# Three edits to a two-block convolution kernel: how a band table reaches both halves of SBUF, when the first normalisation reads its PSUM bank, and where three tables are cleared

## The chip, the cores and the metric

The kernel runs on one core of a Trainium2 chip. The metric is the device time of one execution in microseconds (us). The kernel before takes 5860.17 us, the median of three runs (5853.47 to 5860.35 us). All arithmetic is in 32-bit floats.

## The reference

The input `x` has 8 images of 96 x 96 pixels with 192 channels. Two residual blocks follow each other, each behind a group normalisation over 32 groups of 6 channels:

```
def _gn(v, G=32, eps=1e-5):            # per image and group, over rows, columns and 6 channels
    return (g - mean(g)) / sqrt(var(g) + eps)

# block 0: 192 -> 384 channels, 3x3 depthwise, four running averages, layer norm, 384 -> 192
proj  = einsum(_gn(x), W_in) + b_in
local = depthwise_conv3x3(proj, conv_w)
mixed = 0.25*(lr + rl + tb + bt) + local   # s = 0.6*s + 0.4*x along columns and rows, both ways
x = x + einsum(layernorm(mixed), W_out) + b_out

# block 1: 7x7 depthwise, layer norm, 192 -> 768 -> gelu -> 192
y = depthwise_conv7x7(_gn(x), dw_kernel) + dw_bias
y = einsum(gelu(einsum(layernorm(y), w0) + b0), w1) + b1
x = x + y * gamma
```

## The kernel before, in words

The program goes through five stages, A to E. Between them everything lies in HBM (the tensors `P_d`, `M_d`, `X1_d`, `X2_d`, `Y_d`). Inside each stage the order of the instructions on every engine is the order in which the source issues them (`tc.manual_schedule()`); tile pools decide which buffer a tile gets, and an instruction waits until the former user of that buffer is done.

**Stage A** (group norm 0 and the projection). It has 8 images of 12 steps each. A step transposes four pairs of image columns on TensorE (`turn`, L351, three times per step: k = 0, 2, 1), scales them on the way out of PSUM (ScalarE L358 for k = 0 and 2, VectorE L356 for k = 1), multiplies with `W_in` in `project_full` (twelve matmuls, L365) and `project_rest` (twelve, L378), and evicts with the bias (ScalarE L391, VectorE L389). While image b is projected, VectorE collects the statistics of image b+1 (`bn_stats`, L320). In the last steps of an image the statistics are finished by `norm_steps`, whose closures are taken one by one by the table `ends`: `means` in step 9 after `project_full`, `squares` in step 10 after `project_full`, `powers` and `shift` in step 10 after `project_rest`, then `spread` and `keep` in step 11. The small results of `norm_steps` lie in a PSUM bank (`gn_ps`) of the same pool and tag as the transposes (`pt`), and that tag has two banks. `means` writes the bank (L51, L52); it is read at the beginning of `squares` (L57, L59). `squares` writes a bank (L71); it is read at the beginning of `powers` (L75).

Image 0 has nothing to hide behind: its statistics and `norm_steps` run ahead of the first step. In step 3 of image 0 `spread_kernels` builds the band tables of the two depthwise convolutions in SBUF: GpSimd clears `z0`, `z1` and `pad` (L265, L276, L290), VectorE copies the taps in (L267, L284), TensorE transposes the 7x7 taps (L274), VectorE takes them out (L275). In step 4 `store_kernels` stores the three tables on SyncE's queue (L293, L298, L299). The memory of `pad` and its neighbours is used again by stage C's constants, whose first write (`mean_w`, L791, VectorE) therefore waits until the stores have landed.

**Stage B** does the 3x3 convolution by banded matmuls (L582) and the running averages (VectorE scans, L612 and L621). **Stage C** does layer norm and `W_out`, adds the residual, and collects the statistics of group norm 1; it calls the same `norm_steps`, whose closures are there taken one per step, from a pool tag of its own with one bank.

**Stage D** (the 7x7 convolution). Channels are handled in 32 blocks m of 6; an iteration i takes the two blocks 2i and 2i+1. `load_d(m)` brings two things:

- `xin`: three times two transfers of 64 partitions x 6 KB (L753), the even ones (partitions 0 to 63) on SyncE's queue, the odd ones (64 to 127) on GpSimd's;
- `band`: the banded taps, the same 64 rows for both halves of the partitions, so one transfer of 64 partitions x 1248 floats on each queue (L758).

Five blocks fit in SBUF (`ND` = 5), so block m's load waits for the matmuls of block m-5. `scale_d(m)` applies group norm 1 to `xin` in eight VectorE instructions (L1016). `conv_d` does 432 matmuls an iteration (L1031) from both halves of the partitions, and ScalarE evicts (L1042). `store_d` stores the result, partitions 0 to 63 on SyncE's queue and 64 to 127 on GpSimd's (L1068). The order in an iteration i is: store of i-1 on SyncE's queue; loads of blocks 2i+3 and 2i+4; store of i-1 on GpSimd's queue; `scale_d` of 2i+2 and 2i+3; the matmuls of i.

**Stage E** is layer norm and the two dense layers, with the result.

Of the kernel before, what the change touches and what calls it, by code (L numbers as in the profile page):

```python
# [28 lines left out]
    nc.gpsimd.tensor_tensor(out, t, neg_half[:rows, :n], ALU.pow)  # L29


def norm_steps(nc, pool, psum, tag, st, avg, count, neg_half):

    rows, n, k, _ = st.shape
    sub = 2 * k
    sv = st.rearrange("p n k (e t) -> p n (k e) t", t=3)  # L40
    rb = pool.tile([n, 2], F32, tag="gn_rb", name="gn_rb")
    t = {}

    def bank():
        return psum.tile([128, 512], F32, tag=tag, name="gn_ps")

    def means():
        ms = pool.tile([rows, n], F32, tag="gn_ms", name="gn_ms")
        nc.vector.tensor_reduce(ms, sv[:, :, :, 1], AX.X, ALU.add)
        t["ps"] = ps = bank()  # L50
        nc.tensor.matmul(ps[:, :n], avg, ms, start=True, stop=True)  # L51
        nc.tensor.matmul(ps[:n, n : n + 1], ms, avg[:, 0:1], start=True, stop=True)  # L52

    def squares():

        gm = pool.tile([rows, n], F32, tag="gn_gm", name="gn_gm")
        nc.vector.tensor_scalar(gm, t["ps"][:rows, :n], 1.0 / sub, None, ALU.mult)  # L57
        t["mean"] = mean = pool.tile([n, 1], F32, tag="gn_mean", name="gn_mean")
        nc.vector.tensor_scalar(mean, t["ps"][:n, n : n + 1], -1.0 / sub, None, ALU.mult)  # L59
        d = pool.tile([rows, n, sub], F32, tag="gn_d", name="gn_d", bufs=1)  # L60
        nc.vector.tensor_tensor(
            d, sv[:, :, :, 1], gm.unsqueeze(2).to_broadcast([rows, n, sub]), ALU.subtract
        )
        nc.vector.tensor_tensor(d, d, d, ALU.mult)
        nc.vector.scalar_tensor_tensor(
            d, sv[:, :, :, 2], 1.0 / count, d, ALU.mult, ALU.add
        )
        ds = pool.tile([rows, n], F32, tag="gn_ds", name="gn_ds")
        nc.vector.tensor_reduce(ds, d, AX.X, ALU.add)
        t["ps"] = ps = bank()  # L70
        nc.tensor.matmul(ps[:n, 0:1], ds, avg[:, 0:1], start=True, stop=True)  # L71

    def powers():
        ve = pool.tile([n, 1], F32, tag="gn_ve", name="gn_ve")
        nc.vector.tensor_scalar(ve, t["ps"][:n, 0:1], 1.0 / sub, GN_EPS, ALU.mult, ALU.add)  # L75
        nc.gpsimd.tensor_tensor(rb[:, 0:1], ve, neg_half[:n, 0:1], ALU.pow)

    def shift():
        nc.vector.tensor_tensor(rb[:, 1:2], t["mean"], rb[:, 0:1], ALU.mult)

    return [means, squares, powers, shift], rb


@with_exitstack
def conv_blocks_kernel(
# [83 lines left out]
    nc.vector.memset(avg, 1.0 / S)  # L169
    neg_half = const.tile([128, 64], F32, name="neg_half")  # L170
    nc.vector.memset(neg_half, -0.5)
    ones = const.tile([64, 128], F32, name="ones")
    nc.vector.memset(ones, 1.0)


# [47 lines left out]
    with ExitStack() as ph:  # L223
# [14 lines left out]
            nc.scalar.dma_start(bin_, b_in.rearrange("(m p) -> p m", p=128))  # L238


        member = cp.tile([GROUPS, 2, GROUPS, GS], F32, name="member")
        for i in range(2):
            nc.vector.tensor_copy(
                member[:, i],
                ident[:GROUPS, :GROUPS].unsqueeze(2).to_broadcast([GROUPS, GROUPS, GS]),
            )
        memberf = member.rearrange("p i g s -> p (i g s)")

# [6 lines left out]
        pad = zp.tile([S, D * WV * B // S], F32, name="pad")  # L255

        def load_kernels():
            nc.sync.dma_start(
                k0.rearrange("p m a b -> p m (a b)"),
                conv_w.rearrange("(m p) o a b -> p m (o a b)", p=128),  # L260
            )
            nc.sync.dma_start(k1, dw_kernel.rearrange("a b o c -> (a b) (o c)"))

        def spread_kernels():
            nc.gpsimd.memset(z0, 0.0)  # L265
            for m in range(NC):
                nc.vector.tensor_copy(  # L267
                    z0[:, m, :, RB - 1 : RB + 2],
                    k0[:, m],
                )  # L270
            kps = ps_t.tile([128, 512], F32, tag="pt", name="kps")
            for i in range(2):
                half = kps[:S, i * 64 : i * 64 + 49]
                nc.tensor.transpose(half, k1[:, i * S : (i + 1) * S], ident[:49, :49])  # L274
                nc.vector.tensor_copy(k1t[:, i].rearrange("p a b -> p (a b)"), half)  # L275
            nc.gpsimd.memset(z1, 0.0)  # L276
            for i in range(2):
                for p in range(PH):
                    for d in range(3):

                        kw = d * PH + p - 2
                        lo, hi = max(0, -kw), min(PH, 7 - kw)
                        if lo < hi:
                            nc.vector.tensor_copy(  # L284
                                z1[:, i, p, d * ZS + ZO : (d + 1) * ZS].rearrange(
                                    "c (t e) -> c t e", e=PH
                                )[:, :, lo:hi],
                                k1t[:, i, :, kw + lo : kw + hi],
                            )
            nc.gpsimd.memset(pad, 0.0)  # L290

        def store_kernels():
            nc.sync.dma_start(  # L293
# [21 lines left out]
        def stats_a(b):  # L315

            st = sp.tile([S, GROUPS, NK, 6], F32, tag="gn_st", name="gn_st")

            def step(k, g):
                nc.vector.bn_stats(  # L320
                    st[:, g, k],
                    xq[b * NK + k].rearrange("p j w c -> p (j w) c")[:, :, g * GS : (g + 1) * GS],
                )

            last, rb = norm_steps(nc, sp, ps_t, "pt", st, avg, NJ * WA * GS // 2, neg_half)
            cols = sp.tile([128, 3, 2], F32, tag="cols", name="cols")
            held = []

            def spread():
                ps = ps_t.tile([128, 512], F32, tag="pt", name="ps_col")  # L330
                for k, lo in enumerate((0, 128, DH)):
                    nc.tensor.matmul(
                        ps[:, 2 * k : 2 * k + 2],
                        memberf[:, lo : lo + 128],
                        rb,
                        start=True,
                        stop=True,
                    )
                held.append(ps)

            def keep():
                nc.vector.tensor_copy(cols.rearrange("p k a -> p (k a)"), held[0][:, 0:6])

            bn = [lambda k=k, g=g: step(k, g) for k in range(NK) for g in range(GROUPS)]
            return bn, last + [spread, keep], cols
# [394 lines left out]
    def load_d(m):  # L740
        c = m * HC
        row = D * WV * B
        pool = d_pools[m % ND > 0]
        xin = pool.tile([128, NT, BP, HC, 2 * WV], F32, tag="xin", name="xin")

        for t in range(NT):
            for g, eng in enumerate((nc.sync, nc.gpsimd)):
                src = bass.AP(
                    tensor=X1_d.tensor,
                    offset=X1_d.offset + (2 * t + g) * HG * PH * row + c * WV * B,  # L750
                    ap=[[row, 64], [1, HC * WV * B]],
                )
                eng.dma_start(  # L753
                    xin[g * 64 : (g + 1) * 64, t].rearrange("q a c n -> q (a c n)"), src
                )
        band = pool.tile([128, HC, ZW], F32, tag="band", name="band1")
        for g, eng in enumerate((nc.sync, nc.gpsimd)):
            eng.dma_start(  # L758
                band[g * 64 : (g + 1) * 64].rearrange("q c l -> q (c l)"),
                Z2_d[:, c : c + HC].rearrange("r c l -> r (c l)"),  # L760
            )
        return band, xin

    s1 = s1_pool.enter_context(tc.tile_pool(name="s1", bufs=1)).tile(
# [2 lines left out]
    with ExitStack() as ph:  # L767
# [108 lines left out]
        def group_steps(x1c, k, i):  # L876
# [16 lines left out]
            steps = [bn[j : j + per] for j in range(0, len(bn), per)]  # L893
            if n < NH * NS - 1:
                return steps
            last, rb = norm_steps(nc, sp, ps_s, "gn_ps", st, avg, GS * WC // NS // 2, neg_half)
            held = []

            def spread():

                dg = sp.tile([2 * GROUPS, 2, 2 * GROUPS], F32, tag="gn_dg", name="gn_dg", bufs=1)
                for a in range(2):
                    nc.vector.tensor_scalar(
                        dg[:, a],
                        ident[: 2 * GROUPS, : 2 * GROUPS],
                        rb[:, a : a + 1],
                        None,
                        ALU.mult,
# [1 line left out]
                ps = ps_s.tile([128, 512], F32, tag="gn_ps", name="ps_s1")  # L910
                nc.tensor.matmul(
                    ps[:, : 4 * GROUPS],
                    ones[: 2 * GROUPS],
                    dg.rearrange("p a g -> p (a g)"),
                    start=True,
                    stop=True,
# [81 lines left out]
    with ExitStack() as ph:  # L998
# [9 lines left out]
                dw_bias.rearrange("(i k c) -> k i c", k=2, c=HC)[k].partition_broadcast(64),  # L1008
            )

        def scale_d(m, xin):
            xv = xin.rearrange("q t a c (v b) -> q t a c v b", b=2)
            for b in range(B):
                sc, sh = (s1[:, a, b % 2, b // 2, m : m + 1] for a in range(2))
# [59 lines left out]
        with tc.manual_schedule():  # L1074
            loads = [first_d] + [load_d(m) for m in range(1, 3)]
            make_weights(ps_y.tile([128, 512], F32, tag="py1", name="ps_b0"))
            for m in range(2):
                scale_d(m, loads[m][1])
            done = None
            for i in range(n_i):  # L1080
                pair, loads = loads[:2], loads[2:]
# [7 lines left out]
                    store_d(done, i - 1, 1)  # L1089
                if i + 1 < n_i:  # L1090
                    for k in range(2):
                        scale_d(2 * i + 2 + k, loads[k][1])
                done = op.tile([128, NB, BP * NV, HC, 2 * WQ], F32, tag="yo", name=f"yo_{i}")
                for c in range(HC):
                    conv_d(pair, c, done, i)
# [248 lines left out]
```

## Time and profile before

The profiled execution took 5861.74 us and has a span of 5860.0 us, so 1.7 us lie around the span. The stages below are stretches of its span; PE busy is TensorE's busy time, DMA the mean busy share of the core's 16 DMA engines, clock the share of TensorE's clock that was granted.

| stage | stretch, us | PE busy, us | clock | DMA | GB/s |
|---|---|---|---|---|---|
| A | 45 to 783 | 714.0 | 0.99 | 0.84 | 245 |
| B | 798 to 1831 | 1025.1 | 0.99 | 0.91 | 236 |
| C | 1831 to 2874 | 1015.5 | 0.99 | 0.92 | 272 |
| between C and D | 2874 to 2904 | 8.3 | 0.50 | 0.88 | 268 |
| D, first iteration | 2904 to 2950 | 27.9 | 0.73 | 0.93 | 265 |
| D, loads running | 2950 to 3336 | 331.4 | 0.93 | 1.00 | 322 |
| D, end | 3336 to 3400 | 46.8 | 0.89 | 0.68 | 212 |
| E, start | 3400 to 3460 | 28.9 | 0.66 | 0.58 | 130 |
| E | 3460 to 5860 | 2392.1 | 1.00 | 0.26 | 69 |

How to read it: where PE busy is close to the stretch, TensorE sets the pace and only what stands in its queue counts; where it is not, and the DMA share is 1.00, the transfers set it. Matmuls are pipelined, so a busy TensorE need not be at its peak. In the lines further down "PE", "PEld", "DVE", "ACT", "POOL" and "SPq" are TensorE's matmuls, its weight loads, VectorE, ScalarE, GpSimd and SyncE's queue; the numbers in front are the start and the busy time in us; the bracket gives the idle time before, and what ended it. KB are 1024 bytes.

### The profile page before, as it was taken

The page shows a single profiled execution, that of the slowest core. Times are in us where ns is not written, and L with a number is a line of the kernel's source. Part 1 is how long each engine was busy: PE and PEld are TensorE (multiplying, and loading weights), DVE is VectorE, ACT ScalarE, POOL GpSimd, SP SyncE. Part 2 cuts the span into 40 slices and gives each one's busy share as a digit, 9 for nine tenths or more (in the row PEclk, how much of TensorE's full clock was granted, in tenths as well). Part 3 has the DMA queues.
Part 4 walks back from the last instruction along what each step waited for, and adds up shares of the span by engine and source line. Part 5 has one row for each costly group of instructions (what it writes and reads, how often), then busy time and mean ns, then how long its engine had stood idle before and what let it go on. Part 6 is the DMA issues. An engine that isn't in the chain of part 4 may idle for free.

```text
span 5860.0 us, 123059 instructions
## 1 busy us (share of the span) xinstructions
PE 5592.6 (95%) x48550; PEld 3974.4 (68%) x48550; DVE 3452.2 (59%) x8023; ACT 2426.3 (41%) x6146; POOL 2560.5 (44%) x2731
## 2 busy tenths in 40 slices
PE   6999989999998999999688869999999999999999
PEld 3655533333335999999677757777777777777777
DVE  5556459999996777777633234444444444444443
ACT  2444447777775666666344422222222222222222
POOL 1111138888886777777422223333333323333322
PEclk9999989999999999999899989999999999999999
DMA  7999879999997999999899942323222232323221
GB/s 206 275 286 257 233 202 244 243 243 243 244 244 207 268 276 282 277 282 276 255 316 327 298 120 60 80 65 81 64 68 74 64 81 65 80 65 78 63 64 40
DMA packets 634284, 1054.50 MB, mean 180 GB/s; under 512 B 108683, under 2 KB 509284, under 8 KB 633708
## 3 DMA queue, kind: packets, MB, share of 16 engines
q1 hardware_dynamic: 516924, 620.81, 40.4%
q0 software_dynamic: 110656, 423.20, 22.6%
q8 instruction: 385, 6.31, 0.5%
q10 hardware_dynamic: 6128, 2.61, 0.2%
q14 instruction: 191, 1.56, 0.1%
HBM read 585.19 MB, written 476.72 MB: 181 GB/s over the span
## 4 chain that ended last, share of the span: by engine, by line
PE 77%; DMA 6%; issue 1%; DVE 1%; SPq 1%; POOL 1%; ACT 0%; POOLq 0%; ACTq 0%; DVEq 0%
PE po L1233 19%; PE po L835 13%; PE hp L1203 13%; PE pl L582 10%; PE hp L1213 7%; PE pa L603 5%; PE pt L833 4%; DMA xin<-X_d 2%; PE pa L606 2%; PE py L1031 2%; PE pt L1186 2%; DMA Y_d<-yo 2%; DMA band<-Z_d 1%; DMA X_d<-x1c 0%; SPq L1068 0%
## 5 line engine op out<-in xcount | busy, mean ns | idle before, releaser
L1222 ACT ACTIVATE g<-hp,b0g 128x384 f32<-128x384 f32 x1152 | 563.3, 587 | 1834.3 <-PE hp L1213 1834.3
L1233 PE MATMUL po<-w1g,g 128*128 128x192 f32 x6912 | 1162.6, 327 | 0.0
L1233 PEld LDWEIGHTS po<-w1g,g 128*128 128x128 f32 x6912 | 1121.5, 190 | 1.1 <-issue 1.1
L835 PE MATMUL po<-wc,mt 128*96 128x193 f32 x4608 | 883.5, 327 | 0.0
L1190 DVE COPY yT<-pt 128x384 f32<-128x384 f32 x288 | 248.5, 863 | 1043.9 <-PE pt L1186 1043.5
L1203 PE MATMUL hp<-yT,w0w 128*128 128x384 f32 x2304 | 781.8, 489 | 0.4 <-DVE yT L1190 0.4
L1251 POOL DMA_DIRECT2D out_dram<-xo x576 | 342.6, 597 | 878.3 <-DVE xo L1240 863.5
L835 PEld LDWEIGHTS po<-wc,mt 128*96 128x96 f32 x4608 | 713.1, 164 | 3.2 <-DVE x1u L858 0.5
L582 PE MATMUL pl<-pin,band 34*32 34x380 f32 (+1 forms) x13824 | 629.8, 489 | 18.9 <-DMA pin<-P_d 18.5
L1203 PEld LDWEIGHTS hp<-yT,w0w 128*128 128x128 f32 x2304 | 429.6, 191 | 257.5 <-issue 3.7
L612 DVE TENSOR_TENSOR_SCAN z<-decay,loc 128x768 f32<-128x768 f32 x288 | 505.8, 1756 | 60.5 <-ACT loc L591 30.8
L652 POOL TENSOR_TENSOR mo<-mo,z 128x768 f32<-128x768 f32 x288 | 529.7, 1840 | 3.4 <-ACT mo L607 0.4
L29 POOL TENSOR_TENSOR rs<-rs_ve,neg_half 96x8 f32<-96x8 f32 x96 | 159.1, 1657 | 822.6 <-DVE rs_ve L28 804.6
L582 PEld LDWEIGHTS pl<-pin,band 34*32 34x32 f32 x13824 | 232.7, 107 | 397.9 <-issue 397.6
L621 DVE TENSOR_TENSOR_SCAN z<-decay,z 128x768 f32<-128x768 f32 x288 | 498.2, 1730 | 0.0
L1031 PE MATMUL py<-xin,band 63*64 63x248 f32 (+1 forms) x6912 | 406.1, 389 | 81.3 <-DVE xin L1016 50.7
L842 ACT ACTIVATE sq<-pt,mean 96x384 f32<-96x384 f32 x768 | 443.0, 577 | 25.7 <-ACT mean L839 0.8
L1031 PEld LDWEIGHTS py<-xin,band 63*64 63x64 f32 x6912 | 348.5, 140 | 138.6 <-DVE xin L1016 40.1
L603 PE MATMUL pa<-loc,mix 128*32 128x384 f32 x3456 | 431.9, 493 | 0.0
L606 PE MATMUL pa<-last,down 96*32 96x384 f32 x1152 | 426.8, 493 | 1.0 <-ACT mo L607 1.0
L1213 PE MATMUL hp<-yT,w0w 64*128 64x384 f32 x2304 | 423.5, 500 | 0.0
L365 PE MATMUL pm<-xT,win 128*128 128x384 f32 x1152 | 397.4, 496 | 5.1 <-DVE po L389 5.1
(116 smaller groups left out, 7623.8 us busy)
## 6 DMA issues: line engine op xcount, KB each, us to landing
P_d<-po POOLq DMA_DIRECT2D x96, 1152.0 KB, 9.9
pin<-P_d SPq DMA_DIRECT2D x192, 576.0 KB
mt<-M_d SPq DMA_DIRECT2D x576, 192.0 KB
xq<-in_x_dram SPq DMA_DIRECT2D x96, 576.0 KB
xr<-in_x_dram SPq DMA_DIRECT2D x384, 144.0 KB
X_d<-x1u POOLq DMA_DIRECT2D x192, 288.0 KB, 4.5
X_d<-x1c SPq DMA_DIRECT2D x192, 288.0 KB
y<-Y_d SPq DMA_DIRECT2D x24, 2304.0 KB
```

The source lines that it names most:

```text
L582: nc.tensor.matmul(pls[g][at * RB : (at + 1) * RB, :, lo:hi], band[rows, c, kh, :], pin[rows, c, :, NJ - 1 - j, lo + kh - 1 : hi + kh - 1] ...
L603: nc.tensor.matmul(pa[at], mix[:, i, at], loc[:, q], start=True, stop=True)
L606: nc.tensor.matmul(pa[at], down[:, to], last[:, q], start=True, stop=True)
L612: nc.vector.tensor_tensor_scan(zf, decay_f, loc.rearrange("p q n -> p (q n)"), 0.0, ALU.mult, ALU.add)
L621: nc.vector.tensor_tensor_scan(zr, decay_f, zr, 0.0, ALU.mult, ALU.add)
L652: nc.gpsimd.tensor_tensor(m, m, z, ALU.add)
L835: nc.tensor.matmul(po[:S, b], lhs[m], wc[:, m], start=(m == 0), stop=(m == NC - 1))
L1031: nc.tensor.matmul(pys[t // 2][g][k * 64 : (k + 1) * 64, t % 2, :, lo:hi], pair[k][0][rows, c, d * ZS : d * ZS + 64], pair[k][1][rows, t, ...
L1203: nc.tensor.matmul(hps[m, q], w0w[:, 2 * q, m * 128 : (m + 1) * 128], yT[:, 2 * q], start=True, stop=False,)
L1213: nc.tensor.matmul(hps[m, q], w0w[p, 1, m * 128 : (m + 1) * 128], yT[p, 1], start=False, stop=True,)
L1222: nc.scalar.activation(g[:, m, q], hps[m, q], AF.Gelu, bias=b0g[:, m : m + 1], scale=1.0)
L1233: nc.tensor.matmul(po[:, q], g[:, m, q, k * 128 : (k + 1) * 128], w1g[:, m], start=(m == 0), stop=(m == NE - 1),)
```

## The change

1. **Band rows.** `load_d(m)` issues one band transfer in place of two: into partitions 0 to 63 on SyncE's queue where m is even, into 64 to 127 on GpSimd's queue where m is odd. The other half of the partitions is filled by one VectorE copy at the head of `scale_d(m)`.
2. **`norm_steps`.** The reading of the bank becomes closures of its own (`take_means`, `take_squares`). With `at_once` they run directly behind the matmuls that fill the bank (stage A); without it they run where they ran before (stage C). Besides, the small tiles get 128 rows or columns in place of 32 or 64 (`rb`, `ms`, `ds`, `mean`, `ve`, `member`, `ones`, `gn_dg`), with the unused columns of `ms` and `ds` cleared by two VectorE memsets; the instructions that read them are 128 wide.
3. **Tables.** The three GpSimd memsets of `z0`, `z1` and `pad` move from `spread_kernels` (step 3 of image 0) to `load_kernels`, which is issued ahead of image 0's statistics.

```diff
     def means():
-        ms = pool.tile([rows, n], F32, tag="gn_ms", name="gn_ms")
-        nc.vector.tensor_reduce(ms, sv[:, :, :, 1], AX.X, ALU.add)
-        t["ps"] = ps = bank()
-        nc.tensor.matmul(ps[:, :n], avg, ms, start=True, stop=True)
-        nc.tensor.matmul(ps[:n, n : n + 1], ms, avg[:, 0:1], start=True, stop=True)
+        ms = pool.tile([rows, 128], F32, tag="gn_ms", name="gn_ms")
+        nc.vector.memset(ms[:, n:], 0.0)
+        nc.vector.tensor_reduce(ms[:, :n], sv[:, :, :, 1], AX.X, ALU.add)
+        ps = bank()
+        nc.tensor.matmul(ps[:, :n], avg, ms[:, :n], start=True, stop=True)
+        nc.tensor.matmul(ps[:, n : n + 1], ms, avg[:, 0:1], start=True, stop=True)
+        t["ps"] = ps
+
+    def take_means():
+        ps = t["ps"]
+        t["gm"] = gm = pool.tile([rows, n], F32, tag="gn_gm", name="gn_gm")
+        nc.vector.tensor_scalar(gm, ps[:rows, :n], 1.0 / sub, None, ALU.mult)
+        t["mean"] = mean = pool.tile([128, 1], F32, tag="gn_mean", name="gn_mean")
+        nc.vector.tensor_scalar(mean, ps[:, n : n + 1], -1.0 / sub, None, ALU.mult)
...
-    return [means, squares, powers, shift], rb
+    both = lambda *fs: lambda: [f() for f in fs]
+    if at_once:
+        return [both(means, take_means), both(squares, take_squares), powers, shift], rb
+    return [means, both(take_means, squares), both(take_squares, powers), shift], rb
...
         def load_kernels():
+            for z in (z0, z1, pad):
+                nc.gpsimd.memset(z, 0.0)
...
         def spread_kernels():
-            nc.gpsimd.memset(z0, 0.0)
...
-            nc.gpsimd.memset(z1, 0.0)
...
-            nc.gpsimd.memset(pad, 0.0)
...
         band = pool.tile([128, HC, ZW], F32, tag="band", name="band1")
-        for g, eng in enumerate((nc.sync, nc.gpsimd)):
-            eng.dma_start(
-                band[g * 64 : (g + 1) * 64].rearrange("q c l -> q (c l)"),
-                Z2_d[:, c : c + HC].rearrange("r c l -> r (c l)"),
-            )
+
+        g = m % 2
+        (nc.sync, nc.gpsimd)[g].dma_start(
+            band[g * 64 : (g + 1) * 64].rearrange("q c l -> q (c l)"),
+            Z2_d[:, c : c + HC].rearrange("r c l -> r (c l)"),
+        )
         return band, xin
...
-        def scale_d(m, xin):
+        def scale_d(m, band, xin):
+            g = m % 2
+            nc.vector.tensor_copy(
+                band[(1 - g) * 64 : (2 - g) * 64], band[g * 64 : (g + 1) * 64]
+            )
             xv = xin.rearrange("q t a c (v b) -> q t a c v b", b=2)
```

## The prediction

> **What bounds the kernel now.** I read the page's slices first, then a table of stretches, then for each edit the view of its own place.
>
> ```profile
> PE   6999989999998999999688869999999999999999
> DMA  7999879999997999999899942323222232323221
> ```
>
> Each digit is a 40th of the span (146.5 us). TensorE is at 9 nearly everywhere; the dip "68886" (2784 to 3516 us) takes in stage D and its two borders, and there the DMA row reads "89994": full in D proper. So stages A, B, C, E are paced by TensorE and D is not. The stretches put numbers on it:
>
> ```profile
> 45.00:783.00 738.00, 714.03 (x3548) 433.03 (x3548) 382.19 (x1312) 314.12 (x577) 111.25 (x134) 0.99 0.84 245
> 2950.00:3336.00 386.00, 331.35 (x5644) 277.86 (x5640) 122.77 (x207) 160.68 (x313) 110.86 (x207) 0.93 1.00 322
> ```
>
> The columns after the length are busy us of PE, PEld, DVE, ACT, POOL, then clock, DMA share and GB/s. In A an edit counts if it shortens TensorE's queue. In D it counts if it takes bytes away: the share is 1.00 at 322 GB/s for 386 us.
>
> **Part 1, the band rows.** What the transfers of that D stretch are:
>
> ```profile
> xin<-X_d POOLq DMA_DIRECT2D x77, 384.0 KB, 14.3
> band<-Z_d POOLq DMA_DIRECT2D x26, 312.0 KB, 16.4
> band<-Z_d SPq DMA_DIRECT2D x26, 312.0 KB
> ```
>
> Of 52 band transfers in the stretch 26 go. 26 x 312 x 1024 bytes = 8.31 MB, and at 322 GB/s that is **25.8 us**. The gain holds while the engines stay full, so I ask what the edit adds to the waits.
>
> ```profile
> DVE xin L1016 <- DMA Y_d<-yo: 153.7, 13, 20.7
> DVE xin L1016 <- DMA xin<-X_d: 112.8, 14, 21.8
> POOL Y_d L1068 <- DMA xin<-X_d: 89.0, 48, 4.5
> ```
>
> Columns: us in total, times, longest. VectorE waits for transfers 266 us of the 496 that this answer covers (2905 to 3400), so a copy has room. Its price: no copy of 64 x 1248 is in the trace. Nearest contiguous row: L724, 128x768 in 0.61 us, so 0.61 x 1248/768 = 0.99 us; the strided copy L871, 96x768 in 1.05 us, would give 1.7. I take 1.0 (both sides are contiguous). 32 copies are 32 us of VectorE. They are hidden behind those waits; without that cover two copies an iteration would cost 2 us each time, 30 in all.
>
> The new wait: `scale_d` now begins with an instruction that needs `band`, and all eight L1016 and the next block's stand behind it. When does a band land?
>
> ```profile
> 3083.05 0.52 POOL L1068 DMA_DIRECT2D Y_d<-yo  x1 [2.30 <-DMA xin<-X_d]
> 3085.24 0.51 POOL L1068 DMA_DIRECT2D Y_d<-yo  x1 [1.66 <-DMA band<-Z_d]
> ```
>
> These two issues are released by block 13's last `xin` and its `band` on POOL's queue, 2.2 us apart; VectorE starts block 13's L1016 only at 3089.04, on SyncE's `xin`, since SyncE's queue has a store ahead of the load. An odd block has its band on POOL's queue, so its copy is done 3 us before VectorE could scale anyway. An odd block is the one that the next iteration waits for (it is loaded in the iteration just before). An even block's band follows its `xin` on SyncE's queue by some 2.2 us, so VectorE is 3.2 us later there; but that block was loaded one iteration earlier, and its L1016 (3096.66) ran 27 us before those of the odd one (3123.26). So both delays lie beside the wait for the next load. Only the first iteration has no such slack: block 1's L1016 started at 2918.38 with the landing of `xin`, matmuls followed at 2923.22. Now band (+2.2 us) and copy (+1.0) come first, less 0.3 MB taken from the transfers before: block 0's second band, 1.2 us at the 268 GB/s of the stretch before D. Net 2.0 us later, between 0 and 3.2. After the last load (3336 on) nothing changes.
>
> [...] The row: every `xin` transfer here is already a 64-partition one, and the mix runs at 322 GB/s with share 1.00[...], so I take 26. [...] The rows: POOL's issues in D themselves wait on landings of earlier transfers (89.0 us for L1068 on `xin` alone) with others in flight, so a hold of 1 us delays nothing that the engines lack. I take 0.
>
> D: -25.8 + 2.0 = **-24 us** (bounds -33, all 32 transfers at 310 GB/s, to +3).
>
> **Part 2, the norm's bank in A.** The timeline at the end of image 0's twelve steps:
>
> ```profile
> 128.94 2.21 PE L378 MATMUL pm<-xT,win 64*128 64x384 f32 x12
> 137.11 0.55 PE L351 MATMUL pt<-ident,xq 96*128 96x96 f32 x4 [0.81 <-ACT xT L358]
> 137.59 2.21 PE L378 MATMUL pm<-xT,win 64*128 64x384 f32 x12
> 145.62 0.55 PE L351 MATMUL pt<-ident,xq 96*128 96x96 f32 x4 [0.81 <-ACT xT L358]
> 146.10 2.21 PE L378 MATMUL pm<-xT,win 64*128 64x384 f32 x12
> 154.18 2.21 PE L378 MATMUL pm<-xT,win 64*128 64x384 f32 x12
> 161.36 2.21 PE L378 MATMUL pm<-xT,win 64*128 64x384 f32 x12
> ```
>
> L378 comes once a step: 8.65, 8.51, 8.08, then the usual 7.18 us. The three steps with norm work cost 3.7 us more. In two of them the second group of transposes waits 0.81 us for ScalarE to read the first: one bank of the tag's two is held by `gn_ps`, so both groups use the other. Read at once, the bank is free by about 136.2 (L52 ends at 135.82, two reads of 0.18 and 0.14 us), as the transposes that need it come up at 136.1: the first wait falls to 0.0 to 0.1 us, the second, with one read, to 0. VectorE, which must now wait for TensorE inside step 9, had been idle 4.85 us before L389, which was ready only at 139.19. In step 10 the matmul L71 needs VectorE's chain: it ended 1.0 us before TensorE came to L71, and stays there (the two reads go from its head, a memset of 0.14 us, as L196, comes in). So 1.55 us per image. The 128-wide forms: the weights of L71 and L332 in their narrow form are loaded 0.1 us late behind L365, wider ones hold 0.08 us more; I take 0.2 us gain over both, bounds -0.2 to +0.4. Per image 1.75, and seven images run so: **-12 us** (bounds -9 to -15). Image 0's own norm has no cover: two memsets, +0.2. In C three images pay +0.1 and win +0.1 for the wider forms: 0.
>
> **Part 3, the tables.** Step 3 of image 0:
>
> ```profile
> 77.95 0.30 DVE L267 COPY z<-k 128x9 f32<-128x9 f32 x3 [2.17 <-POOL z L265]
> 78.42 0.24 PE L274 MATMUL kps<-ident,k 49*96 49x49 f32 x1 [4.14 <-DVE k1t L275]
> 81.34 1.32 SPq L299 DMA_DIRECT2D X_d<-pad  x1
> 93.51 0.17 DVE L791 MEMSET mean_w<- 128x128 f32 x1 [10.97 <-DMA X_d<-pad]
> ```
>
> GpSimd's memsets stand behind its four stores of step 2, VectorE waits 2.17 us for the first, TensorE for VectorE. Moved to an idle GpSimd, that goes; the memsets themselves (0.61, 1.48, 0.54 us) cost nothing there, since POOL is idle until 44.46. But what is late next is `mean_w`: it waits for the store of `pad`, and TensorE stops from 89 to 94.16 for the eviction behind it. So the gain is how much sooner the store lands. It is issued 2.5 us sooner, but the engines are full from 69 to 90 us (share about 1.0 in 1-us stretches) with the same bytes: between 0 and 2.5, I take **-1.5**.
>
> **Sum.** -24 - 12 + 0.2 - 1.5 = -37.3. From the profiled 5861.7 that is 5824.4; that execution lies 1.6 us above the median of the runs, so from 5860.2: **5823 us**.
>
> **The rivals.** (a) *The engines stop being full in D*: loads wait for matmuls of five blocks before, and with a later VectorE the queue may run dry; then part 1 gives only its +2. For it: the start already runs dry (share 0.93 at 2904 to 2950). Against: matmuls take 331 of 386 us, partly at half clock after a wait. -13 + 2: 5849. [...] (c) *All of it and more*: D by 32 and no loss at the start, A by 15, tables 2.5: 5811. (d) *Slower*: the copy at the head of `scale_d` is late in every iteration, as VectorE takes its blocks in order. Price: 2.2 us for the even band and two copies, 4.2 us, times 15 is 63, less 13: 5910. It decides once VectorE's lateness exceeds what is still queued at an iteration's end, some 7 us (iteration 6's matmuls ended at 3124.4, and block 16's `xin` was still landing until 3131.17), against 3 to 4 here.
>
> **How the numbers follow.** Main case 0.66; (a) 0.07, (b) 0.11, (c) 0.12, (d) 0.04. The main case alone is 5812 to 5834. The range goes from 5808, below (c), to 5841, past (b); (a) and (d), 0.11, and about as much on the edges stay out. A change below 0.2% (11.7 us, about what a measurement of this kernel can tell from none) comes only from part of (a): 0.03; slower is (d) with a rest: 0.04; faster 0.93.
>
> **What would show it.** Right: in D the band rows halved, L1016 still waiting for `xin` and stores, 2950 to the last load shorter by some 26 us at the same 320 GB/s; the copy near 1 us; steps of about 7.8, 7.5 and 8.0 us where 8.65, 8.51 and 8.08 stood; no wait of L267, `mean_w` at about 92. Wrong: GB/s in D below 310[...], a DMA share below 0.95 with VectorE waiting for `band` (a, d), POOL's issues longer than 0.51 us in the copies' time, or `mean_w` still at 93.5.

## The result, and the profile after

The changed kernel takes 5810.95 us (median of 4 runs, 5809.23 to 5812.43) against 5860.26 us of the kernel before, a ratio of 0.9918 with a 95% interval of 0.9901 to 0.9935: about 48 us faster, between 38 and 58. Forecast was 5823, 37 us faster. The profiled execution took 5809.23 us, its span 5807.5. Set against the span before (5860.0), the milestones put the 52.5 us in three places: when C's last matmul ends the changed kernel is 15.4 us ahead, from there to E's first matmul it gains 33.2, and in E and its last stores 4.0. (E is 2426 to 2430 us long in every trace below, whatever was changed, so these 4 us belong to no edit.)

The slices of the page first:

```profile
PE   6999989999998999999789869999999999999999
DMA  7999779999997999999899842323232222323221
```

TensorE's dip is shallower ("78986" where "68886" stood), and the DMA row falls off one slice sooner ("998423" where "999423" stood). The stretches, with the columns of the prediction (us of PE, PEld, DVE, ACT, POOL, then clock, DMA share, GB/s):

```profile
45.00:768.00 723.00, 706.91 (x3548) 433.00 (x3548) 383.21 (x1326) 313.00 (x577) 109.78 (x132) 0.99 0.85 250
2935.00:3284.00 349.00, 314.34 (x5612) 275.59 (x5606) 139.99 (x225) 163.46 (x313) 109.49 (x197) 0.96 0.99 334
```

The second row is the work that took 386 us before (from the end of the first iteration to the fourteenth). It moves 116.5 MB where it moved 124.2, and at 334 GB/s where it was 322. So between these two traces the bytes are not the whole of it. Its transfers, in the view of DMA issues:

```profile
xin<-X_d POOLq DMA_DIRECT2D x80, 384.0 KB, 12.7
...
band<-Z_d POOLq DMA_DIRECT2D x13, 312.0 KB, 12.5
band<-Z_d SPq DMA_DIRECT2D x13, 312.0 KB
```

Half the band transfers are gone. The copy that stands in for them, in the groups of VectorE's instructions by line (busy us and mean ns, then idle us just before):

```profile
L1030 DVE COPY band<-band 64x1248 f32<-64x1248 f32 x32 | 25.9, 808 | 122.3 <-DMA band<-Z_d 95.7 <-PE py L1052 26.6
```

0.81 us each, where 1.0 was taken. Of the waits in D (the whole of it, from the first matmul of the first iteration to that of the last):

```profile
POOL Y_d L1089 <- DMA xin<-X_d: 103.1, 59, 3.6
DVE band L1030 <- DMA band<-Z_d: 95.7, 24, 13.2
DVE xin L1037 <- DMA Y_d<-yo: 75.3, 9, 10.3
DVE xin L1037 <- DMA xin<-X_d: 48.6, 6, 11.4
```

VectorE waits for the loads as before, under another name: the copy now meets the wait first. And GpSimd's DMA issues are longer in the copies' time, which the prediction had named as a sign of being wrong:

```profile
2947.58 0.81 DVE L1030 COPY band<-band 64x1248 f32<-64x1248 f32 x1 [13.20 <-DMA band<-Z_d]
2947.74 0.76 POOL L1089 DMA_DIRECT2D Y_d<-yo  x1 [1.28 <-DMA band<-Z_d]
2950.07 0.51 POOL L1089 DMA_DIRECT2D Y_d<-yo  x1 [1.58 <-ACT yo L1063]
```

Thirty issues overlap a copy, and 22 of them end 0.10 to 0.12 us after the copy ends, whenever they began. The thirty take 0.75 us in the median, the other 234 of D 0.52. Together this holds GpSimd's queue for some 6 us in the whole of D.

One view the prediction did not have: stretches of one iteration each, four of the fifteen.

```profile
2956.90:2988.50 31.60, 25.72 (x439) 21.54 (x435) 15.96 (x26) 12.59 (x25) 8.49 (x15) 0.89 0.99 350
2988.50:3011.30 22.80, 22.80 (x440) 19.75 (x435) 6.57 (x10) 12.54 (x25) 7.70 (x14) 1.00 0.97 302
3144.90:3176.00 31.10, 25.98 (x443) 22.05 (x438) 15.89 (x26) 12.66 (x26) 8.33 (x15) 0.89 0.99 350
3176.00:3198.80 22.80, 22.80 (x437) 20.13 (x433) 6.41 (x11) 12.54 (x25) 7.95 (x15) 1.00 0.96 307
```

Long and short iterations mostly take turns. In the two short ones shown TensorE is busy for all of 22.8 us at full clock: these are at TensorE's own limit, and no byte less would shorten them. In the long ones it waits 5 to 6 us, and part of its work is at a lower clock. Of the fourteen iterations behind the first, three are 22.8 us long and two 23.6; the others take 25.5 to 31.6.

Stage A, the norm steps of image 0 in TensorE's timeline:

```profile
134.59 0.30 PE L55 MATMUL gn_ps<-gn_ms,avg 96*128 96x32 f32 x2
134.73 0.36 PE L56 MATMUL gn_ps<-avg,gn_ms 96*128 96x1 f32 x2
134.95 1.10 PE L367 MATMUL pt<-ident,xq 96*128 96x96 f32 x8
135.98 2.21 PE L394 MATMUL pm<-xT,win 64*128 64x384 f32 x12
...
142.54 0.94 PE L367 MATMUL pt<-ident,xq 96*128 96x96 f32 x8
143.41 2.21 PE L394 MATMUL pm<-xT,win 64*128 64x384 f32 x12
```

All eight transposes are in one row, without the 0.81 us in their middle. The three steps take 7.81, 7.43 and 7.88 us (8.65, 8.51, 8.08 before), the same in all seven images: 2.12 us each, 14.8 in all. And step 3 of image 0, where the tables are used:

```profile
75.60 0.24 PE L292 MATMUL kps<-ident,k 49*96 49x49 f32 x1 [1.88 <-DVE k1t L293]
78.03 1.39 SPq L315 DMA_DIRECT2D X_d<-pad  x1
93.44 0.17 DVE L808 MEMSET mean_w<- 128x128 f32 x1 [14.26 <-DMA X_d<-pad]
94.09 4.78 PE L381 MATMUL pm<-xT,win 128*128 128x384 f32 x8 [9.58 <-DVE po L405]
```

The store of `pad` is issued 3.3 us sooner (78.03 for 81.34), and `mean_w` behind it starts at 93.44 where it started at 93.51. What VectorE no longer waits at the memset it now waits here.

### The profile page after: what moved, and what is told of

The parts are those of the page before. It is cut to its first block, busy times and chain, and to the rows that moved or that the text cites. A ratio compares the mean times of both kernels' runs of the same rounds, so it can differ in the third digit from the quotient of the medians.

```text
span 5807.5 us, 123072 instructions
## 1 busy us (share of the span) xinstructions
PE 5564.8 (96%) x48550; PEld 3970.0 (68%) x48550; DVE 3481.9 (60%) x8079; ACT 2427.7 (42%) x6146; POOL 2555.8 (44%) x2715
## 4 chain that ended last, share of the span: by engine, by line
PE 78%; DMA 4%; DVE 2%; issue 1%; POOL 1%; SPq 0%; ACT 0%; POOLq 0%; ACTq 0%; DVEq 0%
PE po L1254 19%; PE po L852 13%; PE hp L1224 13%; PE pl L598 10%; PE hp L1234 7%; PE pa L619 5%; PE pt L850 4%; PE py L1052 3%; PE pa L622 2%; PE pt L1207 2%; DMA xin<-X_d 2%; DMA Y_d<-yo 2%; DVE xin L1037 1%; DMA band<-Z_d 0%; DMA P_d<-po 0%
## 5 line engine op out<-in xcount | busy, mean ns | idle before, releaser
L1052 PE MATMUL py<-xin,band 63*64 63x248 f32 (+1 forms) x6912 | 389.9, 383 | 62.3 <-DVE xin L1037 44.0
## 6 DMA issues: line engine op xcount, KB each, us to landing
P_d<-po POOLq DMA_DIRECT2D x96, 1152.0 KB, 10.2
```

What stands on the lines that cost most here:

```text
L1052: nc.tensor.matmul(pys[t // 2][g][k * 64 : (k + 1) * 64, t % 2, :, lo:hi], pair[k][0][rows, c, d * ZS : d * ZS + 64], pair[k][1][rows, t, ...
```

## The experiments

Times are medians. Since single executions of one kernel differ by up to 19 us either way from its median, two lengths out of the traces stand beside them. *A* is from the first to the last matmul of L394 (723.7 us before, 708.8 after). *D* is from the first matmul of D's second iteration to the first of its last, fourteen iterations (413.9 us before, 374.7 after); its first iteration is 40 to 43 us long in every trace. Its last one, where delays of the others can still end up, is 23 to 36 us; where this matters, all sixteen are given too (from D's first matmul to the end of its last, 481.0 us before, 444.8 after).

**Part 1 alone: half bands and the copy, in the kernel before**

```diff
-        for g, eng in enumerate((nc.sync, nc.gpsimd)):
-            eng.dma_start(band[g * 64 : (g + 1) * 64]..., Z2_d...)
+        g = m % 2
+        (nc.sync, nc.gpsimd)[g].dma_start(band[g * 64 : (g + 1) * 64]..., Z2_d...)
...
-        def scale_d(m, xin):
+        def scale_d(m, band, xin):
+            g = m % 2
+            nc.vector.tensor_copy(band[(1 - g) * 64 : (2 - g) * 64], band[g * 64 : (g + 1) * 64])
```

> The kernel before with part 1 alone (half band loads, copy in scale_d). Theory 'bytes' (the forecast's term): stage D loses 26 transfers at 322 GB/s less the late start, 24 us, so about 5836. Theory 'reads' (D goes at the pace of its loads, 77.5 MB read in 386 us, so each MB read less is 5.0 us): about 35 to 37 us, so about 5824. If stage D's gain in the changed kernel leaned on an earlier or steadier arrival from stage A, it is smaller than 36 here.

5824.16 us against 5855.37 beside it, ratio 0.9946 (0.9934 to 0.9959): 32 us faster, 24 to 39. D is 375.6 us, as in the full change (374.7), so A's earlier end lends D nothing. The forecast's 24 us lies at the edge of the interval. Theory 'reads' had this time right, but it fails in the run with more stores below; this run alone cannot say why the gain is more than forecast.

**Parts 2 and 3 alone: both band loads, no copy**

```diff
-        g = m % 2
-        (nc.sync, nc.gpsimd)[g].dma_start(band[g * 64 : (g + 1) * 64]..., Z2_d...)
+        for g, eng in enumerate((nc.sync, nc.gpsimd)):
+            eng.dma_start(band[g * 64 : (g + 1) * 64]..., Z2_d...)
...
-            nc.vector.tensor_copy(band[(1 - g) * 64 : (2 - g) * 64], band[g * 64 : (g + 1) * 64])
```

> The changed kernel without part 1: both halves of each band loaded, no copy (parts 2 and 3 alone). Theory 'bytes' (what part 1 gives is the transfers that go): stage D as long as in the kernel before, and as in the run with both loads and the copy within its noise of 6 us; 14 to 17 us below the kernel before, about 5841. Rival 'order' (the copy, by moving VectorE's and so TensorE's waits, makes the same transfers run at 333 instead of 322 GB/s): 10 to 12 us longer than the run with both loads and the copy, about 5851.

5845.82 us, ratio 0.998 (0.9971 to 0.9989): 12 us faster, 6 to 17; A is 708.8. The stretch of D:

```profile
2931.10:3337.40 406.30, 354.36 (x6053) 306.98 (x6050) 131.51 (x221) 173.76 (x337) 117.44 (x220) 0.94 0.99 324
```

This is the code that D had before, and D takes 406.3 us, 7.6 less than in the one trace of the kernel before:

```profile
2948.80:3362.70 413.90, 355.49 (x6056) 300.57 (x6047) 131.72 (x222) 172.95 (x337) 118.04 (x220) 0.93 0.99 318
```

The changed kernel's first trace, for comparison:

```profile
2934.10:3308.80 374.70, 338.09 (x6055) 297.85 (x6048) 148.00 (x239) 175.62 (x337) 115.33 (x207) 0.96 0.98 328
```

So of the 39 us by which the traces of before and after differ in D, some 8 may be the spread of single executions, and so may part of the rise in GB/s.

**Both loads and the copy**

```diff
-        g = m % 2
-        (nc.sync, nc.gpsimd)[g].dma_start(band[g * 64 : (g + 1) * 64]..., Z2_d...)
+        for g, eng in enumerate((nc.sync, nc.gpsimd)):
+            eng.dma_start(band[g * 64 : (g + 1) * 64]..., Z2_d...)
```

> The changed kernel with both halves of every band loaded again, and the copy kept (over the half that the second load brought). Stages A and the tables stay as changed, 15 to 17 us below the kernel before. Theory 'reads' or 'bytes': D is back at the length of before, plus up to 3 us at the start, so 5844 to 5848. Rival 'order' (the extra gain of D comes from VectorE's work being later or differently placed, not from bytes): D still 8 to 12 us shorter than before, so about 5833. Rival 'the copy costs': each iteration waits for both band landings and the copy; over 5855.

5840.78 us, ratio 0.9973 (0.996 to 0.9985), 3 us under the range that theories 'reads' and 'bytes' gave.

```profile
2938.30:3340.50 402.20, 345.45 (x6053) 301.47 (x6050) 155.90 (x252) 176.38 (x337) 122.83 (x220) 0.93 0.98 327
```

402.2 us with the copy, 406.3 without: the copy and its wait cost nothing that can be seen, and a gain from them is within the spread. The rival "order" wanted 10 to 12 us; the lengths differ by 4 and the medians by 5, so most or all of what D gains comes with the transfers that go. The two runs with both loads (mean 404.3) against the nine traces with one load per band (368.5 to 375.6, mean 372.9): 31.4 us. In this stretch 54 band transfers were issued in the one and 27 in the other. So 27 transfers, 8.63 MB, were worth 31.4 us, 1.16 each, where 322 GB/s make 0.99 of it and 26.8 in all (29.3 by the one run, 33.4 by the other, 41.0 by the trace of the kernel before: above it in each). Over all sixteen iterations, though, D is 468.0 us with the copy and 479.0 without, against 442.9 in the mean of the nine (437.8 to 450.5): 25.1 and 36.1 us. The medians of the two runs lie 30 and 35 us above the changed kernel's 5810.95. So the transfers that go were worth 25 to 36 us by the measure taken, mostly more than their bytes at the mixed rate; that they were worth more is likely, not certain.

**Nearly no band loads**

```diff
+        if m >= ND:
+            return bands[m % ND], xin
         band = pool.tile([128, HC, ZW], F32, tag="band", name="band1")
+        bands.append(band)
...
-            nc.vector.tensor_copy(...)
+            if m < ND:
+                nc.vector.tensor_copy(...)
```

> The changed kernel, where blocks 5 to 31 load no band and make no copy, but use the band of the block five before (so the depthwise kernels of those channels are wrong: their values are left out, the work on TensorE is the same). 27 transfers of 0.32 MB less, 8.6 MB. Theory 'bytes' at 334 GB/s: 26 us, about 5785. Theory 'reads' (4.97 us a MB read): 43 us, about 5768. Rival 'TensorE is next': the gain stops once matmuls are the bound, below 15 us, over 5796.

5805.52 us (5792.89 to 5814.32), ratio 0.9906 (0.9891 to 0.9922). D:

```profile
2951.00:3318.70 367.70, 337.20 (x6056) 229.93 (x6048) 129.71 (x216) 176.42 (x337) 104.31 (x193) 0.95 0.92 310
```

The first 27 transfers were worth 31.4 us; the 27 that go here are worth 5.2 (372.9 to 367.7), or 10 over all sixteen iterations (442.9 to 433.0). The rival "TensorE is next" stands for part of the time: the DMA share falls to 0.92, TensorE's busy time stays where it was (337), and six of the fourteen iterations are at 22.8 to 23.3 us. But TensorE is idle for 30 of the 367.7 us, and seven iterations still take 28.5 to 30.9; what bounds those is not shown.

**More bytes written instead of read**

```diff
             eng = (nc.sync, nc.gpsimd)[k]
+            eng.dma_start(
+                EX_d[2 * i + k],
+                yo[k * 64 : (k + 1) * 64].rearrange("r b a c n -> r (b a c n)")[:, :1248],
+            )
```

> The changed kernel with one more store per block in D: 64 rows of 4992 bytes of yo to a buffer of their own, on the queue that stores the block, 32 x 0.32 MB = 10.2 MB written more (the same sizes as the band loads). Theory 'bytes' at 334 GB/s: 30 us slower, about 5841. Theory 'reads' (writes go beside the reads): 0 to 10 us slower, 5811 to 5821.

5833.03 us, ratio 0.9955 (0.994 to 0.997), 22 us above the changed kernel.

```profile
2939.90:3329.60 389.70, 343.31 (x6053) 304.21 (x6048) 149.38 (x241) 176.11 (x337) 123.32 (x221) 0.94 0.98 338
```

29 such stores are issued in this stretch, 9.3 MB, and lengthen it by 16.8 us (372.9 to 389.7), 1.8 us a MB. The loads above cost 3.6 us a MB. Over all sixteen iterations a MB stored costs 1.9 us (460.9 against 442.9) and a MB loaded 2.9 and 4.2; by the medians, for all 32 transfers of 10.2 MB, 2.2 and 2.9 to 3.4. Both theories miss: a byte written is not free, but it costs less than a byte read, about half to two thirds of it by these measures, from one run with more stores. So the mean rate of the mix, which the forecast used, was most likely too cheap for loads. Why is open: in D of the changed kernel's trace VectorE waits 144.3 us for loads (95.7 and 48.6) and 75.3 us for stores, but no run here separates what such waits cost from what the bytes themselves cost.

**The bank held as before, with the wide forms**

```diff
-norm_steps(nc, sp, ps_t, "pt", st, avg, NJ * WA * GS // 2, neg_half, True)
+norm_steps(nc, sp, ps_t, "pt", st, avg, NJ * WA * GS // 2, neg_half, False)
```

> The changed kernel, with the first pass's norm results read one step later as before, from 128-wide forms. Theory 'bank' (the forecast's): the two 0.81 us stalls of an image come back, 7 x 1.55 = 10.9 us, and the wide forms keep 0.5 us an image, so about 5822. Rival 'wide forms': the gain of 2.1 us an image comes mostly from the wide tiles, then no more than 5 us comes back, below 5816.

5823.68 us, ratio 0.995 (0.9937 to 0.9964). The stalls are back in TensorE's timeline:

```profile
137.73 0.53 PE L367 MATMUL pt<-ident,xq 96*128 96x96 f32 x4
139.06 0.55 PE L367 MATMUL pt<-ident,xq 96*128 96x96 f32 x4 [0.81 <-ACT xT L374]
...
147.44 0.55 PE L367 MATMUL pt<-ident,xq 96*128 96x96 f32 x4 [0.81 <-ACT xT L374]
```

The three steps are 8.60, 8.38 and 7.89 us. Against the changed kernel that is 1.75 us an image for the bank, 12.3 in seven; against the kernel before it is 0.37 an image for the wide forms, 2.6. The two sum to A's 14.9.

**The memsets back in their old steps**

```diff
         def load_kernels():
-            for z in (z0, z1, pad):
-                nc.gpsimd.memset(z, 0.0)
...
         def spread_kernels():
+            nc.gpsimd.memset(z0, 0.0)
```

(The memsets of `z1` and `pad` return to their old lines too.)

> The changed kernel with its three memsets back in the steps before. Theory 'the landing decides' (mean_w waits for the store of pad, whose landing did not move): within 1 us of the changed kernel, 5811. Rival (the forecast's term): 1.5 to 2.5 us slower, 5812.5 to 5813.5.

5809.75 us, ratio 0.9924 (0.991 to 0.9937): no slower than the changed kernel. Image 0's steps 2 and 3 together take 27.7 us here and 28.8 in the kernel before, and 28.6 in the changed kernel and when it was profiled again. Part 3 moves a wait from one step to the next and gives nothing.

**The store of `pad` sooner**

```diff
             nc.sync.dma_start(k1, dw_kernel.rearrange("a b o c -> (a b) (o c)"))
+            nc.sync.dma_start(X1_d[S * PH]..., pad)
...
         def store_kernels():
-            nc.sync.dma_start(X1_d[S * PH]..., pad)
```

> The changed kernel with the store of pad issued in the prologue, behind the loads of the kernels' weights, instead of in step 4 of the first image. Theory 'the landing decides': mean_w and the eviction behind it no longer wait 14 us for a store behind full queues, TensorE's gap from 84.5 to 94.1 us goes, so 8 to 9.6 us faster than the changed kernel, about 5802. Rival: the gap stays, since the next buffer or load waits for the store of z1 or z0 in the same full queues; then 0 to 2 us, about 5810.

5812.07 us, ratio 0.9936 (0.9919 to 0.9952): nothing gained, and the timeline says why.

```profile
93.99 0.17 DVE L808 MEMSET mean_w<- 128x128 f32 x1 [13.17 <-DMA Z_d<-z]
```

The rival holds: `mean_w` then waits for the store of `z1`, which stands behind the first results' 3.5 MB (three transfers of 1152 KB) in the same full queues (DMA share 0.97 to 1.02 from 75 to 90 us in the changed kernel's trace). All of the prologue's stores have to be gone before those results.

**Tables spread and stored sooner**

```diff
-        rest = {3: spread_kernels, 4: store_kernels}
+        rest = {0: spread_kernels, 1: store_kernels}
```

> The changed kernel with the tables spread in step 0 of the first image and stored in step 1 (before: steps 3 and 4), while the DMA engines are idle. Theory 'full queues' (moving the store of pad alone gained nothing, since mean_w then waited for the store of z1, which stood behind the 3.5 MB of the first results; all of the prologue's stores must go ahead of them): TensorE's gap of 9.6 us shrinks to 0 to 3 us, so 6 to 9 us faster than the changed kernel, about 5802 to 5805. Rival: VectorE now comes to mean_w within some 3 us of the stores' issue and to lnb within some 6 us, and waits for their landing and for the load of gb there: gain 0 to 4 us.

5798.78 us, ratio 0.9912 (0.9899 to 0.9925).

```profile
53.29 0.40 SPq L315 DMA_DIRECT2D X_d<-pad  x1
57.51 0.39 SPq L800 DMA_DIRECT2D wo<-in_L_conv_W_out_dram  x1
```

The stores go out at 50 to 53 us, a stretch in which the DMA share of the changed kernel's trace is 0.00 (49.5 to 57.5 us), and have landed by 57.5; VectorE waits 3.63 us for `pad` there, in time that TensorE does not need. Image 0's first eight steps are all 7.18 us, and A is 694.5 us, 14.3 shorter: more than the 6 to 9 expected, since the 2.5 us that step 2 had too long go as well. With steps 1 and 2 in place of 0 and 1:

> The same with steps 1 and 2. Theory 'full queues': the stores are issued at about 68 us, 5 us ahead of the first results' stores, and beside 1.8 MB of loads; mean_w at about 80 finds its place free, but gb, loaded behind it, lands only with the first results (90 us or later), so a shorter gap at lnb: gain 3 to 8 us. Rival: the stores still land with the first results at 93 us, gain 0.

5814.76 us, ratio 0.9923 (0.9908 to 0.9938). In the profiled execution A is 701.3 us, 7.5 shorter than in the changed kernel: one gap became two smaller ones.

```profile
82.09 0.17 DVE L808 MEMSET mean_w<- 128x128 f32 x1 [2.22 <-DMA X_d<-pad]
...
93.31 0.45 DVE L813 COPY lnb<-gb 128x96 f32<-128x96 f32 x3 [5.63 <-DMA gb<-in_L_conv_ln_b_dram]
```

The theory named the wait at `lnb` and its cause. The gain does not show in this kernel's median. In its profiled execution, 5815.35 us, it was lost at the start of B, as described below: from A's end to B's last eviction it took 1059 us.

**The changed kernel and the sooner tables, on one chip**

> The changed kernel itself, beside the kernel with the tables spread and stored two or three steps sooner. About 5811; stage D between the last of C's matmuls and the first of E's 516 to 523 us, if the lengths of the runs with half the band loads so far (516 to 522) are the spread of one kernel.

> The kernel with the tables spread in step 0 and stored in step 1 of the first image, against the changed kernel on the same chip. Theory 'full queues' (its trace: stage A 14 us shorter, VectorE's wait for the store of pad 3.6 us where it hides): 10 to 14 us faster than the changed kernel, about 5799. Rival: what A gains is lost at the start of B, which was 10 us longer in that trace at a lower granted clock; then 0 to 4 us.

The changed kernel took 5813.9 us (ratio 0.9918, 0.9905 to 0.9932), the sooner tables 5801.16 us (0.99, 0.9886 to 0.9914): 12.7 us between the medians, as in the first pair (12.2), though the two intervals just overlap. D of the changed kernel was 368.5 us this time, but from C's last matmul to E's first it was 525.7, where the expectation had 516 to 523: the spread of one kernel is wider than that. Of ten executions with the sooner tables seven took 5795 to 5804 us and three 5811 to 5815. The two profiled ones are among the longer three, and both show the rival's loss beside the theory's gain: A is 14.3 us shorter, and the time from A's end to B's last eviction 1054 and 1056 us where the changed kernel has 1042 and 1044. The clock says where it went. First the changed kernel (its first trace), then the sooner tables, stretches of 10 us around the start of B:

```profile
780.00:790.00 10.00, 4.48 (x60) 1.77 (x68) 0.00 (x0) 0.23 (x1) 0.00 (x0) 0.50 0.64 157
790.00:800.00 10.00, 10.00 (x135) 3.84 (x126) 6.99 (x5) 4.76 (x12) 0.49 (x2) 0.50 0.95 192
800.00:810.00 10.00, 10.00 (x146) 2.80 (x136) 7.74 (x5) 5.17 (x13) 3.24 (x5) 0.77 0.85 175
810.00:820.00 10.00, 10.00 (x192) 3.48 (x184) 9.70 (x7) 7.29 (x18) 5.52 (x7) 1.00 0.88 192
```

```profile
770.00:780.00 10.00, 5.58 (x72) 2.23 (x80) 0.44 (x1) 1.34 (x4) 0.00 (x0) 0.50 0.66 140
780.00:790.00 10.00, 10.00 (x130) 3.61 (x118) 7.65 (x5) 3.68 (x10) 0.74 (x3) 0.50 0.87 177
...
810.00:820.00 10.00, 10.00 (x112) 2.77 (x112) 5.65 (x4) 5.10 (x12) 2.39 (x4) 0.57 0.28 64
820.00:830.00 10.00, 10.00 (x192) 3.42 (x184) 8.78 (x6) 6.58 (x16) 5.88 (x7) 1.00 0.73 152
```

Between A and B TensorE is idle for 12.57 us and, after two matmuls, for 6.21 more (in the changed kernel's first trace), and its clock is granted at 0.50 afterwards, until about 805 us in the one and 819 in the other. It is no matter of records alone: the stretch at 0.57 holds 112 matmuls, the next, at 1.00, 192. The low clock comes in two lengths. From the moment when B's matmuls follow each other without a gap it lasts 18 to 20 us in ten of the fourteen traces, the kernel before and the changed kernel among them, and 44 to 51 in four. Those four are the three with earlier tables and the run with nearly no band loads, where it ends at 838 us. A and B of that run are those of the changed kernel, so the earlier tables are not needed for the longer one; whether they make it more frequent is not shown. What sets the length stays open, and the unprofiled executions have no trace that would show theirs. The version with the sooner tables is the fastest here that does all the work; no edit was tried against the low clock.

## Why the prediction was right, and by how much it was off

The direction was right, and 5811 lies inside the range of 5808 to 5841, 3 us from its lower end and just below the 5812 to 5834 of the main case. The likeliest case, 5823, is 12 us off: D gave some 6 us more than forecast (by its fourteen iterations), A 3 more, the tables 1.5 less, and the other 4 lie within the spread of executions. The mechanisms of D and A held; their sizes did not. The time is that of rival (c), "all of it and more", with D's and A's gain as (c) had them, but without its 2.5 us for the tables.

*D, "26 of 52 band transfers go, 8.31 MB at 322 GB/s = 25.8 us; first iteration +2.0".* This is the term that came out too small, most likely in its price. The count holds (27 in the fourteen iterations), but the rate is that of loads and stores together, and a load was worth more than the mean: 1.16 us in place of 0.99, 31.4 us in all by the fourteen iterations, 25 to 36 by all sixteen. The first iteration began 1.1 us late, not 2.0 (from C's last matmul to D's first it is 39.6 us in the mean of the nine traces, 38.5 before). So part 1 is worth about 30 us by these lengths and 32 (24 to 39) by its own run, where 24 was forecast, at the edge of that interval. The traces of before and after differ by more, since the one of before was long.

*"The copy is hidden; price 1.0 us".* Right: 0.81 us, and with or without it D takes 402.2 or 406.3 us. The new wait for `band`, 96 us of VectorE's time, replaced waits for the same loads.

*The price of a half band.* 25 to 36 us were measured for the transfers that go, where the mixed rate gives 26.8: with two queues writing to opposite halves (DMA share 0.98 to 1.00 at 318 to 334 GB/s in D), a 64-partition transfer taken away was worth about its bytes at the mixed rate or more. Rival (b), a smaller gain from D, rested on nothing that the trace of before shows, and did not come.

*The hold of GpSimd's queue*, which the prediction set at 0, is there: 22 of the 30 issues that meet a copy end 0.10 to 0.12 us behind it, and the prediction's sign for it came true (0.75 us in the median). But it comes to some 6 us of GpSimd's queue, and no cost shows when the copy is added to the same loads (402.2 us with it, 406.3 without).

*A, "1.75 us an image, 12 us".* Measured 2.12 and 14.8. The bank gave 1.75, where 1.55 was read off the two waits of 0.81; the wide forms gave 0.37, where 0.2 was taken. The step times forecast (7.8, 7.5, 8.0) came as 7.81, 7.43, 7.88.

*Tables, "-1.5".* Wrong, at the low end of its bounds: about 0, with `mean_w` at 93.44 where about 92 was forecast and 93.5 named as the sign of being wrong. The prediction had both facts, that `mean_w` waits for the store of `pad` and that the engines are full with the same bytes when it is issued (share 0.97 to 1.02 from 78 to 90 us in the changed kernel's trace), and still gave 1.5 of the 2.5 us of the earlier issue to the landing. Issued 3.3 us sooner behind the same bytes, the store landed at the same time.

*Rival (a)*, that the engines stop being full, did not come true here, but its limit is near: three of the fourteen iterations are now at TensorE's 22.8 us, and taking the other half of the band loads away gave 5 to 10 us. *Rival (d)*, the copy late in every iteration, did not come true at all.

## What to carry to other kernels

Where a stage is paced by its transfers, price those that go by adding or removing some of the same direction, not by the mean rate of the mix (in D a MB written cost 1.8 to 2.2 us and a MB read 2.9 to 4.2, where 322 GB/s make 3.1); and stop where an iteration's length equals its matmul time (22.8 us here), for there the next byte was worth little (5 to 10 us for the 27 transfers taken out last, with six of fourteen iterations at 22.8 to 23.3 us, where those taken out first gave 25 to 36). A store issued sooner gained here only where it came ahead of what fills the queues: 3.3 us sooner behind the same bytes it left `mean_w` where it was (93.44 and 93.51), 25 us sooner with its whole set it had landed by 57.5. So move the whole set to a stretch where the queues are not full, not one member, and look which sibling is waited for next. One trace of a transfer-bound stage may be off by some two per cent of that stage (413.9 and 406.3 us for the same code of D), so a rate that seems to change with an edit is first to be measured twice on the same code.

## What the runs showed of the hardware

In D a MB more written cost 1.8 to 2.2 us and a MB more read 2.9 to 4.2, by the measure taken, both in transfers of 0.32 MB with rows of 4992 bytes, the DMA share at 0.98 to 0.99 in both.

A DMA issue of GpSimd that met one of VectorE's 0.81 us copies mostly ended 0.10 to 0.12 us after the copy (22 of 30 in the changed kernel's trace). The 30 took 0.75 us in the median where others took 0.52.

Between A and B, where TensorE idled for 12.57 and then 6.21 us in the changed kernel's trace, its clock was granted at 0.50, and it stayed so for 18 to 20 or 44 to 51 us of matmuls without a gap, in the fourteen traces until 803 to 838 us. At the start of D the time at 0.50 was shorter: in the first iteration of the changed kernel's trace matmuls start again at 2909, after 15.62 us without one, and the clock is 0.50 until 2914 and 1.00 from there, 5 us later. Why B's start differs is not shown. The two lengths move the time from A's end to B's last eviction by 10 to 17 us (1041 to 1044 or 1054 to 1059), as much as an edit of this size.
